# Scores and weighted values made for two steps together, and the depthwise sums moved from PSUM to SBUF, in a two-layer convolution and attention kernel

## The chip, the core and the metric

The kernel runs on one NeuronCore of one Trainium2 chip. The core has five engines that run their own instruction queues in order: TensorE (PE, matmuls[...]), VectorE (DVE), ScalarE (ACT), GpSimd (POOL) and SyncE (SP, which here issues transfers). The metric is device time in microseconds, median of several runs; lower is better. All arithmetic is in float32.

## What is computed

The input is 8 images of 256 channels and 64 x 64 pixels. Two layers follow each other, each with a group norm ahead of it and a residual add behind it:

```python
x = x + _L0_conv_ref(_gn(x), ...)   # three 1x1 convolutions; two more make 9 weights per pixel and group of
                                    # 8 channels; out = sum over the 9 taps of weight * shifted third map
x = x + _L1_conv_ref(_gn(x), ...)
```

The second layer, around which the change lies, is

```python
att = softmax(einsum(q, unfold7x7(k) + position))          # 4 heads of 64 channels, 49 neighbours of each pixel
out_att = einsum(att, unfold7x7(v))
wts = softmax(einsum('oc,bchw->bohw', Wfc, x) as 9 weights per channel and pixel)
hid = relu(dwconv3x3(x, w1)); oc = dwconv3x3(hid, w2)      # depthwise
out_conv = sum over the 9 of oc * wts
return rate1 * out_att + rate2 * out_conv
```

`oc` is the same for all nine weights. The nine weights sum to one up to rounding; the kernel computes them and their quotient as written.

## The kernel before

**Tiling.** An image is cut into 8 bands of 8 rows (512 pixels). Channels are in two tiles of 128 partitions (`ct`). The main loop (L985) runs over all 64 bands, `g`, and in each band over 8 steps, `s` = (`ct`, `m`) with `m` = 0 to 3. Layer 0 runs ahead: beside layer 1 of band g, layer 0 works on bands g + 9 to g + 12, and its first 12 bands are made alone, with g < 0. In the last ten bands or so, layer 0 has nothing left to do.

**Order.** The order of every queue is the order in which the program text calls the operations (`manual_schedule`, L963). `advance()` moves a counter by one, six times a step, and runs what `after(n, f)` has put off by n such moves. `beside(g, s)` says which operations of layer 0, of the queries, keys and values and of the next band go into the middle or the end of a step.

**A step of layer 1** (L991 to L1039):
- Attention is made in tiles of 8 x 8 queries, two tiles and two heads per step, against 14 x 14 keys. `scores` (L694) makes 8 PE matmuls (L703) of 64 rows, 64 columns and 196 keys into `sco`, a PSUM tile of two banks, one per head. DVE adds the mask and takes the row maximum (L712); ACT makes exponentials with row sums (L720); DVE takes the reciprocal (L727); ACT scales (L729). One step later PE transposes these probabilities (`transposed`, L735) and ACT copies them to SBUF (L737). Another step later 16 small PE matmuls (`weighted_values`, L747) multiply them with the values. Their result, 128 columns, lies in the same `sco` tile as the new step's scores, in columns 256 to 383 of the first bank. `add_values` (L757, DVE) adds it to the output rows.
- `branch_weights` (L825) makes two of the eight weight differences of the nine-fold softmax (the ninth is taken off beforehand, L200): four PE matmuls 128 x 128 x 512 and, on ACT, two exponentials (L830). POOL sums them over the steps (L1026). After the fourth step `dynamic_sum` (L832) divides by the sum and multiplies with `oc` (POOL: L838, L855 to L857; DVE: L845, L846, L850).
- The depthwise convolutions are nine taps each. ACT makes the middle tap (L773, L802) and DVE adds the eight others, each an instruction `sum = input * weight + sum` over one band (L782, L808), two in the first half of a step and two in the second. `m` = 0 and 1 do the first convolution, 2 and 3 the second. The sum `acc` is a PSUM tile of one bank. `relu` (L788) and the scaling by rate2 (L818, `depthwise_end`), both on ACT, bring it to SBUF (`hid`, `oc`). In bands with i = 0 the first row is made apart, with taps of its own.

**Layer 0 beside it.** For each of 9 taps, DVE multiplies a PSUM tile of weights with a map (L460), and POOL adds the product (L468). `hidden_maps` (L409) has a convolution of its own on PE (L429), in two parts, put off by 13 and 19 moves.

**PSUM.** [...] `sco` 2, `acc` 1, and 5 for all else (`gen`).

Of the kernel before, what the change touches and what calls it, by code (L numbers as in the profile page):

```python
# [10 lines left out]
F32 = mybir.dt.float32  # L11
# [75 lines left out]
def conv_layers_kernel(ctx: ExitStack, tc: tile.TileContext, ins: dict, out: bass.AP):  # L87
# [77 lines left out]
        nc.vector.tensor_scalar(bq[:, ct : ct + 1], chan[:, ct, CBQ : CBQ + 1], HD**-0.5, None, ALU.mult)  # L165

    rate1, rate2 = rowp[:, RR1 : RR1 + 1], rowp[:, RR2 : RR2 + 1]
    bv = const.tile([P, NCT], F32, name="bv")
    for ct in range(NCT):
        nc.vector.tensor_mul(bv[:, ct : ct + 1], chan[:, ct, CBV : CBV + 1], rate1)  # L170
# [44 lines left out]
    def after(n, f):  # L215
        later.append((place[0] + n, f))
# [103 lines left out]
    def small_maps(b, i):  # L320


        im = images[b]

        p12 = ps.tile([P, R // 2, W], F32, tag="gen", name=f"p12_{b}_{i}", bufs=5)
        for kt in range(NCT):
            for u in range(2):
                nc.tensor.matmul(
                    p12[64 * u : 64 * u + 64], im.w12s[:, kt, :],
                    im.xc[i][:, kt, u * BAND // 2 : (u + 1) * BAND // 2],  # L330
                    start=(kt == 0), stop=(kt == NCT - 1),
                )
        return lambda: write_maps(b, i, p12)
# [360 lines left out]
    def scores(b, i, ct, m, sco):  # L694


        im = images[b]
        qb, kb = im.qb[i, ct], im.kb[i, ct]
        nm = f"{b}_{i}_{ct}_{m}"
        for t in range(2):  # L700
            for h in range(2):
                c0 = (2 * m + t) * TQ
                nc.tensor.matmul(  # L703
                    sco[half[t], h, :NKEY], qb[half[h], 2 * m + t].rearrange("p r c -> p (r c)"),
                    kb[half[h], :, c0 : c0 + KW], start=True, stop=True,
                )

        prob = probs[turn[0] % len(probs)]
        turn[0] += 1
        nmax = w1.tile([P, 2], F32, tag="nmax", name=f"nmax_{nm}", bufs=4)  # L710
        for h in range(2):
            nc.vector.tensor_tensor_reduce(  # L712
                prob[:, h, :NKEY], sco[:, h, :NKEY], mask, -1.0, 3.0e38, ALU.add, ALU.min, nmax[:, h : h + 1]
            )
        return prob, nmax

# [20 lines left out]
        nc.scalar.copy(pt, ptp)  # L737
        return pt

    def weighted_values(b, i, ct, m, pt, sco):  # L740
        im = images[b]
        po = sco[:, 0, 256 : 256 + 2 * NQ].rearrange("p (r c) -> p r c", r=R)
        for t in range(2):
            for ch in range(2):
                n = min(R, WP - (i + ch) * R) * KW
                for h in range(2):
                    nc.tensor.matmul(  # L747
                        po[half[h], :, t * TQ : (t + 1) * TQ],
                        im.vt[i + ch, m][:n, t, (2 * ct + h) * HD : (2 * ct + h + 1) * HD],
                        pt[:n, h, ch, t * NQ : (t + 1) * NQ],  # L750
                        start=(ch == 0), stop=(ch == 1),
                    )
        return po

    def add_values(b, i, ct, m, po):
        x = images[b].xr[i][:, ct].rearrange("p (r c) -> p r c", r=R)[:, :, 2 * m * TQ : 2 * (m + 1) * TQ]
# [3 lines left out]
    def depthwise_begin(b, i, ct):  # L760


        im = images[b]
        r0 = i * R
        nm = f"{b}_{i}_{ct}"
        yp = im.yp[i]
        lo, hi = (r0 + 1 if i else 0), min(r0 + R + 1, H)
        hid = im.hid[i, ct] = w1.tile([P, R + 2, W], F32, tag="hid1", name=f"hid1_{nm}", bufs=3)
        if i:
            nc.scalar.copy(hid[:, 0:2], im.hid[i - 1, ct][:, R : R + 2])  # L770
        for ra0, rb0 in ((lo, lo + 1), (lo + 1, hi)) if i == 0 else ((lo, hi),):
            acc = ps.tile([P, R, W], F32, tag="acc", name=f"acc1_{nm}_{ra0}")
            nc.scalar.activation(  # L773
                acc[:, : rb0 - ra0], yp[:, ct, PAD + ra0 - r0 : PAD + rb0 - r0], AF.Copy,
                scale=chan[:, ct, CW1 + 4 : CW1 + 5],
            )

            def tap(k, acc=acc, ra0=ra0, rb0=rb0):
                ra, rb, ca, cb = taps(ra0, rb0, k // 3, k % 3)
                o = acc[:, ra - ra0 : rb - ra0, ca:cb]  # L780
                dr, dc = k // 3 - 1 + PAD - r0, k % 3 - 1
                nc.vector.scalar_tensor_tensor(  # L782
                    o, yp[:, ct, ra + dr : rb + dr, ca + dc : cb + dc],
                    chan[:, ct, CW1 + k : CW1 + k + 1], o, ALU.mult, ALU.add,
                )

            def relu(acc=acc, ra0=ra0, rb0=rb0):
                nc.scalar.activation(hid[:, ra0 - r0 + 1 : rb0 - r0 + 1, :], acc[:, : rb0 - ra0], AF.Relu)  # L788

            ks = [k for k in range(KK) if k != 4 and taps(ra0, rb0, k // 3, k % 3)[0] < taps(ra0, rb0, k // 3, k % 3)[1]]  # L790
            if rb0 < hi:
                for k in ks:
                    tap(k)
                relu()
        return [lambda k=k: tap(k) for k in ks], relu

    def depthwise_middle(b, i, ct):

        r0 = i * R
        hid = images[b].hid[i, ct]  # L800
        acc = ps.tile([P, R, W], F32, tag="acc", name=f"acc2_{b}_{i}_{ct}")
        nc.scalar.activation(acc, hid[:, 1 : R + 1, :], AF.Copy, scale=chan[:, ct, CW2 + 4 : CW2 + 5])  # L802

        def tap(k):
            ra, rb, ca, cb = taps(r0, r0 + R, k // 3, k % 3)
            o = acc[:, ra - r0 : rb - r0, ca:cb]
            dr, dc = k // 3 - r0, k % 3 - 1
# [5 lines left out]
        return [lambda k=k: tap(k) for k in range(KK) if k != 4], acc  # L813

    def depthwise_end(b, i, ct, acc):

        oc = w1.tile([P, BAND], F32, tag="oc", name=f"oc_{b}_{i}_{ct}")
        nc.scalar.activation(oc, acc.rearrange("p r c -> p (r c)"), AF.Copy, scale=rate2)  # L818
        return oc

    def branch_weights(b, i, ct, m, j, ex):

# [46 lines left out]
    def beside(g, s):  # L869
# [93 lines left out]
    with tc.manual_schedule():  # L963
# [21 lines left out]
        for g in range(-AHEAD, B * NB):  # L985
            b, i = divmod(g, NB)
            for s in range(STEPS):
# [1 line left out]
                mid, end = beside(g, s)  # L989
                steer(g, s)  # L990
                if g >= 0:  # L991
                    if s == 0 and g + AHEAD < B * NB:
                        mid.append(small_maps(*divmod(g + AHEAD, NB)))
# [6 lines left out]
                    pending = [] if before is None else [(before[:-1], transposed(nm, before[-1]))]  # L1000
# [22 lines left out]
                if g >= 0:  # L1023
                    branch_weights(b, i, ct, m, 1, ex)
                    if exb is not None:
                        after(4, lambda ex=ex, exb=exb: nc.gpsimd.tensor_add(ex, ex, exb))  # L1026
                    if m == 1:
                        conv[1]()
                        conv = depthwise_middle(b, i, ct)
                    if m == NT // 2 - 1:  # L1030
                        oc = depthwise_end(b, i, ct, conv[1])
                        after(4, lambda a=(b, i, ct, ex, oc): dynamic_sum(*a))
                if s % 4 == 3 and 0 <= (g * NCT + ct + 1) < B * NB * NCT:
                    gn, cn = divmod(g * NCT + ct + 1, NCT)
                    conv = depthwise_begin(*divmod(gn, NB), cn)
# [2 lines left out]
                    f()  # L1038
                advance()  # L1039
        for last in (before, None):  # L1040
            sco = score_tile(f"end{last is None}")
            weighted = [(a, weighted_values(*a, pt, sco)) for a, pt in pending]
            for a, po in weighted:
# [86 lines left out]
```

## Time and profile before

| what | value |
|---|---|
| time, median of 3 runs | 4152.74 us (4151.52 to 4157.1) |
| span of the profiled run | 4150.9 us, 72735 instructions |
| ACT | 3081.0 us busy (74%) |
| L825, PE, weight differences | x4096, 1930.5 us busy, 595 ns each |
| L747, PE, weighted values | x8160, 347.0 us busy |
| L703, PE, scores | x4096, 295.2 us busy |
| L782, DVE, first depthwise taps | x1104, 766.2 us busy, 694 ns each |
| L808, DVE, second depthwise taps | x1024, 757.8 us busy, 740 ns each |
| L460, DVE, products of layer 0 | x576, 733.9 us busy, 1281 ns each |
| transfers | 367.89 MB, mean 89 GB/s |

A line of the profile's groups names the source line, the engine, the operation, output and inputs by tile names, shapes, how often it ran, then busy time and mean duration of one, and last the time that the engine was idle just before these instructions, with what ended it. The busy time of a matmul overlaps that of the next, since matmuls are pipelined; what PE really spends per matmul is seen in the starts of the timeline. The duration of an instruction runs from its start on the engine to its end, whatever it did in between.

### The profile page before, as it was taken

The page shows a single profiled execution, that of the slowest core. Times are in us where ns is not written, and L with a number is a line of the kernel's source. Part 1 is how long each engine was busy: PE and PEld are TensorE (multiplying, and loading weights), DVE is VectorE, ACT ScalarE, POOL GpSimd, SP SyncE. Part 2 cuts the span into 40 slices and gives each one's busy share as a digit, 9 for nine tenths or more (in the row PEclk, how much of TensorE's full clock was granted, in tenths as well). Part 3 has the DMA queues.
Part 4 walks back from the last instruction along what each step waited for, and adds up shares of the span by engine and source line. Part 5 has one row for each costly group of instructions (what it writes and reads, how often), then busy time and mean ns, then how long its engine had stood idle before and what let it go on. Part 6 is the DMA issues. An engine that isn't in the chain of part 4 may idle for free.

```text
span 4150.9 us, 72735 instructions
## 1 busy us (share of the span) xinstructions
PE 4022.6 (97%) x25292; PEld 2126.8 (51%) x25292; DVE 3591.9 (87%) x7248; ACT 3081.0 (74%) x7726; POOL 2923.0 (70%) x1902
## 2 busy tenths in 40 slices
PE   6789999999999999999999999999999999999998
PEld 3345555555555555555555555555555555455554
DVE  5878998899898898889998898888988889977777
ACT  3467778777787777877778777777778777687776
POOL 4767777677786777777777777777777677744554
PEclk8999999999999999999999999999999999999999
DMA  8854234234244233334234234244233233111100
GB/s 226 194 135 111 73 91 109 72 94 109 62 101 107 76 94 98 81 94 109 72 85 118 72 94 105 66 101 106 71 82 99 65 87 85 33 41 39 39 28 21
DMA packets 381264, 367.89 MB, mean 89 GB/s; under 512 B 55648, under 2 KB 282720, under 8 KB 380640
## 3 DMA queue, kind: packets, MB, share of 16 engines
q1 hardware_dynamic: 377568, 358.68, 34.3%
q8 instruction: 200, 3.28, 0.3%
q10 hardware_dynamic: 3328, 4.55, 0.3%
q14 instruction: 168, 1.38, 0.1%
HBM read 261.42 MB, written 101.71 MB: 87 GB/s over the span
## 4 chain that ended last, share of the span: by engine, by line
PE 71%; DVE 14%; POOL 6%; ACT 5%; DMA 2%; issue 2%; SPq 1%; POOLq 0%; ACTq 0%; DVEq 0%
PE pf L825 33%; PE ptp L735 5%; PE sco L747 5%; PE pk L658 5%; PE sco L703 5%; PE p L369 5%; DVE prod L460 4%; PE pq L637 4%; POOL xg L468 3%; PE pvt L607 2%; PE pv L563 2%; DVE acc L808 2%; PE pw L447 2%; DVE acc L782 2%; POOL ex L1026 2%
## 5 line engine op out<-in xcount | busy, mean ns | idle before, releaser
L825 PE MATMUL pf<-yp,c_wfc 128*128 128x512 f32 x4096 | 1930.5, 595 | 10.6 <-ACT vc L581 5.0
L468 POOL TENSOR_TENSOR xg<-xg,prod 128x1024 f32<-128x1024 f32 x549 | 1203.9, 2193 | 96.6 <-DVE prod L460 64.1
L825 PEld LDWEIGHTS pf<-yp,c_wfc 128*128 128x128 f32 x4096 | 729.9, 190 | 690.5 <-issue 619.4
L1026 POOL TENSOR_TENSOR ex<-ex,ex 128x1024 f32<-128x1024 f32 x384 | 907.7, 2364 | 61.9 <-ACT ex L830 57.2
L830 ACT ACTIVATE ex<-pf 128x512 f32<-128x512 f32 x1024 | 607.3, 593 | 297.9 <-POOL ex L1026 141.3
L782 DVE SCALAR_TENSOR_TENSOR acc<-yp,c_chan,acc 128x504 f32<-128x504 f32 (+3 forms) x1104 | 766.2, 694 | 42.3 <-ACT acc L773 21.7
L460 DVE SCALAR_TENSOR_TENSOR prod<-pw,c_par,x3q 128x1040 f32<-128x1040 f32 x576 | 733.9, 1281 | 66.8 <-PE pw L447 21.6
L808 DVE SCALAR_TENSOR_TENSOR acc<-hid,c_chan,acc 128x504 f32<-128x504 f32 (+3 forms) x1024 | 757.8, 740 | 20.2 <-ACT acc L802 2.1
L855 POOL TENSOR_TENSOR ex<-ex,rec 128x512 f32<-128x512 f32 x127 | 162.3, 1278 | 809.5 <-DVE rec L850 767.1
L729 ACT ACTIVATE prob<-prob,tot 128x196 f32<-128x196 f32 x1024 | 411.6, 450 | 387.2 <-DVE tot L727 386.4
L712 DVE CUSTOM_DVE_ANT_0 prob<-sco,c_mask 128x196 f32<-128x196 f32 x1024 | 325.5, 355 | 272.4 <-PE sco L703 272.0
L720 ACT ACTIVATE prob<-prob,nmax 128x196 f32<-128x196 f32 x1024 | 461.4, 454 | 46.9 <-DVE nmax L712 45.3
L747 PEld LDWEIGHTS sco<-pt,vt 112*64 112x64 f32 x8160 | 283.8, 137 | 182.3 <-issue 51.7
L737 ACT COPY pt<-ptp 112x512 f32<-112x512 f32 x511 | 297.0, 581 | 105.0 <-PE ptp L735 103.0
L735 PE MATMUL ptp<-ident,prob 128*112 128x128 f32 x2044 | 341.7, 287 | 31.2 <-ACT prob L729 30.5
L747 PE MATMUL sco<-pt,vt 112*64 112x64 f32 x8160 | 347.0, 227 | 0.0
L735 PEld LDWEIGHTS ptp<-ident,prob 128*112 128x112 f32 x2044 | 203.9, 133 | 201.4 <-issue 77.7
L703 PE MATMUL sco<-kb,qb 64*64 64x196 f32 x4096 | 295.2, 357 | 0.0
L563 PE MATMUL pv<-yp,c_wv 128*128 128x512 f32 (+2 forms) x576 | 247.3, 554 | 0.6
L369 PE MATMUL p<-xc,w3s 128*128 128x512 f32 x512 | 244.4, 601 | 0.0
L658 PE MATMUL pk<-yp,c_wk 128*128 128x512 f32 (+2 forms) x576 | 240.8, 545 | 0.0
L637 PE MATMUL pq<-yp,c_wq 128*128 128x512 f32 x512 | 240.6, 592 | 0.0
(140 smaller groups left out, 5294.0 us busy)
## 6 DMA issues: line engine op xcount, KB each, us to landing
x<-x3n SPq DMA_DIRECT2D x128, 264.0 KB, 2.1
x3q<-x SPq DMA_DIRECT2D x128, 264.0 KB, 7.2
xc<-in_x SPq DMA_DIRECT2D x64, 512.0 KB, 5.0
xg<-in_x SPq DMA_DIRECT2D x256, 128.0 KB, 4.8
x<-xg SPq DMA_DIRECT2D x256, 128.0 KB, 2.4
yp<-x SPq DMA_DIRECT2D x128, 256.0 KB, 3.3
xr<-x SPq DMA_DIRECT2D x64, 512.0 KB, 5.8
out_x<-xr SPq DMA_DIRECT2D x64, 512.0 KB, 3.1
```

Of the source, the lines that this page charges most:

```text
L369: nc.tensor.matmul(p3, im.w3s[:, kt, mt * P : (mt + 1) * P], im.xc[i][:, kt, :], start=(kt == 0), stop=(kt == NCT - 1),)
L460: nc.vector.scalar_tensor_tensor(prod[:, :, :RUN], pw[:, j, :RUN].unsqueeze(1).to_broadcast([P, SHARE, RUN]), par[:, PCB2 + k : PCB2 + k + 1],
L468: nc.gpsimd.tensor_add(im.xg[i], im.xg[i], rows(prod))
L703: nc.tensor.matmul(sco[half[t], h, :NKEY], qb[half[h], 2 * m + t].rearrange("p r c -> p (r c)"), kb[half[h], :, c0 : c0 + KW], start=True, ...
L720: nc.scalar.activation(prob[:, h, :NKEY], prob[:, h, :NKEY], AF.Exp, bias=nmax[:, h : h + 1], scale=-1.0, accum_out=tot[:, h : h + 1],)
L735: nc.tensor.transpose(ptp[:, h, ch], prob[:, h, ch * CHUNK : (ch + 1) * CHUNK], ident)
L747: nc.tensor.matmul(po[half[h], :, t * TQ : (t + 1) * TQ], im.vt[i + ch, m][:n, t, (2 * ct + h) * HD : (2 * ct + h + 1) * HD], pt[:n, h, ch ...
L782: nc.vector.scalar_tensor_tensor(o, yp[:, ct, ra + dr : rb + dr, ca + dc : cb + dc], chan[:, ct, CW1 + k : CW1 + k + 1], o, ALU.mult, ALU.add,
L808: nc.vector.scalar_tensor_tensor(o, hid[:, ra + dr : rb + dr, ca + dc : cb + dc], chan[:, ct, CW2 + k : CW2 + k + 1], o, ALU.mult, ALU.add,)
L825: nc.tensor.matmul(pf, wfc[:, kt, 2 * m + j, ct * P : (ct + 1) * P], images[b].yp[i][:, kt, PAD : PAD + R], start=(kt == 0), stop=(kt == N ...
L830: nc.scalar.activation(ex[:, j].rearrange("p (r c) -> p r c", r=R), pf, AF.Exp)
L1026: after(4, lambda ex=ex, exb=exb: nc.gpsimd.tensor_add(ex, ex, exb))
```

## The change

Three things are done together. Scores are made for two steps at once, in every second step: `sco` now holds two times 196 columns per head, and the row maximum of the second step is taken one step later from the same tile. Weighted values are also made for two steps at once, right behind the scores, into a tile `po` of their own. The purpose is fewer switches of PE between kinds of small matmuls. The bank for `po` is got by taking the depthwise sums out of PSUM: they are now summed in SBUF, in `hid` and `oc` themselves, with ReLU in place on `hid`; rate2 is multiplied into the second convolution's weights beforehand, so `depthwise_end` goes. The first row of an image is no longer made apart. In `beside`, the second part of layer 0's hidden convolution is put off by 25 in place of 19 moves, so that it comes ahead of a step with scores.

```diff
+    for ct in range(NCT):
+        nc.vector.tensor_scalar(chan[:, ct, CW2 : CW2 + KK], chan[:, ct, CW2 : CW2 + KK], rate2, None, ALU.mult)
...
-                    sco[half[t], h, :NKEY], qb[half[h], 2 * m + t].rearrange("p r c -> p (r c)"),
+                    score_of(sco, h, m)[half[t]], qb[half[h], 2 * m + t].rearrange("p r c -> p (r c)"),
...
+    def score_of(sco, h, m):
+        return sco[:, h, m % 2 * NKEY : (m % 2 + 1) * NKEY]
...
-        po = sco[:, 0, 256 : 256 + 2 * NQ].rearrange("p (r c) -> p r c", r=R)
+        po = po[:, m % 2]
...
+        po = ps.tile([P, 2, R, 2 * TQ], F32, tag="po", name=f"po_{nm}")
+        return [(a, weighted_values(*a, pt, po)) for a, pt in steps]
...
-            acc = ps.tile([P, R, W], F32, tag="acc", name=f"acc1_{nm}_{ra0}")
...
+        new = hid[:, lo - r0 + 1 : hi - r0 + 1]
+        nc.scalar.activation(
+            new, yp[:, ct, PAD + lo - r0 : PAD + hi - r0], AF.Copy, scale=chan[:, ct, CW1 + 4 : CW1 + 5]
+        )
+        def tap(k):
+            ra, rb, ca, cb = taps(lo, hi, k // 3, k % 3)
+            o = hid[:, ra - r0 + 1 : rb - r0 + 1, ca:cb]
...
+        return [lambda k=k: tap(k) for k in range(KK) if k != 4], lambda: nc.scalar.activation(new, new, AF.Relu)
...
-        acc = ps.tile([P, R, W], F32, tag="acc", name=f"acc2_{b}_{i}_{ct}")
+        oc = w1.tile([P, BAND], F32, tag="oc", name=f"oc_{b}_{i}_{ct}")
+        acc = oc.rearrange("p (r c) -> p r c", r=R)
...
-    def depthwise_end(b, i, ct, acc):
...
-            at = (3, 7, 8, 12, 16) if alone else (5, 13, 14, 19, 21)
+            at = (3, 7, 8, 12, 16) if alone else (5, 13, 14, 25, 27)
...
-                    sco = score_tile(nm)
-                    weighted = [(a, weighted_values(*a, pt, sco)) for a, pt in pending]
-                    prob, nmax = scores(b, i, ct, m, sco)
+                    weighted = []
+                    if m % 2 == 0:
+                        sco = score_tile(nm)
+                        for e in range(2):
+                            scores(b, i, ct, m + e, sco)
+                        weighted, pending = weigh_steps(nm, pending), []
+                        if s == 0 and g + AHEAD < B * NB:
+                            mid.append(small_maps(*divmod(g + AHEAD, NB)))
+                        if before is not None:
+                            pending.append((before[:-1], transposed(nm, before[-1])))
+                    prob, nmax = masked(nm, m, sco)
...
+                    if m % 2:
+                        pending.append((before[:-1], transposed(nm, before[-1])))
```

More of the change, by code (lines that the diff above doesn't have):

```diff
@@ L698, in scores @@
         qb, kb = im.qb[i, ct], im.kb[i, ct]
-        nm = f"{b}_{i}_{ct}_{m}"
         for t in range(2):
@@ L703, in scores, with masked @@
                 nc.tensor.matmul(
-                    sco[half[t], h, :NKEY], qb[half[h], 2 * m + t].rearrange("p r c -> p (r c)"),
+                    score_of(sco, h, m)[half[t]], qb[half[h], 2 * m + t].rearrange("p r c -> p (r c)"),
                     kb[half[h], :, c0 : c0 + KW], start=True, stop=True,
                 )
+    def score_of(sco, h, m):
+        return sco[:, h, m % 2 * NKEY : (m % 2 + 1) * NKEY]
+    def masked(nm, m, sco):
         prob = probs[turn[0] % len(probs)]
@@ L712, in scores @@
             nc.vector.tensor_tensor_reduce(
-                prob[:, h, :NKEY], sco[:, h, :NKEY], mask, -1.0, 3.0e38, ALU.add, ALU.min, nmax[:, h : h + 1]
+                prob[:, h, :NKEY], score_of(sco, h, m), mask, -1.0, 3.0e38, ALU.add, ALU.min, nmax[:, h : h + 1]
             )
@@ L738, in transposed, with weighted_values @@
         return pt
-    def weighted_values(b, i, ct, m, pt, sco):
+    def weighted_values(b, i, ct, m, pt, po):
         im = images[b]
-        po = sco[:, 0, 256 : 256 + 2 * NQ].rearrange("p (r c) -> p r c", r=R)
+        po = po[:, m % 2]
         for t in range(2):
@@ L753, in weighted_values, with weigh_steps @@
         return po
+    def weigh_steps(nm, steps):
+        if not steps:
+            return []
+        po = ps.tile([P, 2, R, 2 * TQ], F32, tag="po", name=f"po_{nm}")
+        return [(a, weighted_values(*a, pt, po)) for a, pt in steps]
     def add_values(b, i, ct, m, po):
@@ L770, in depthwise_begin @@
             nc.scalar.copy(hid[:, 0:2], im.hid[i - 1, ct][:, R : R + 2])
-        for ra0, rb0 in ((lo, lo + 1), (lo + 1, hi)) if i == 0 else ((lo, hi),):
-            acc = ps.tile([P, R, W], F32, tag="acc", name=f"acc1_{nm}_{ra0}")
-            nc.scalar.activation(
-                acc[:, : rb0 - ra0], yp[:, ct, PAD + ra0 - r0 : PAD + rb0 - r0], AF.Copy,
-                scale=chan[:, ct, CW1 + 4 : CW1 + 5],
-            )
[L778 to L795, printed above, removed]
+        new = hid[:, lo - r0 + 1 : hi - r0 + 1]
[5 more added lines that the diff above has]
+            o = hid[:, ra - r0 + 1 : rb - r0 + 1, ca:cb]
+            dr, dc = k // 3 - 1 + PAD - r0, k % 3 - 1
+            nc.vector.scalar_tensor_tensor(
+                o, yp[:, ct, ra + dr : rb + dr, ca + dc : cb + dc],
+                chan[:, ct, CW1 + k : CW1 + k + 1], o, ALU.mult, ALU.add,
+            )
+        return [lambda k=k: tap(k) for k in range(KK) if k != 4], lambda: nc.scalar.activation(new, new, AF.Relu)
     def depthwise_middle(b, i, ct):
@@ L811, in tap @@
             )
-        return [lambda k=k: tap(k) for k in range(KK) if k != 4], acc
-    def depthwise_end(b, i, ct, acc):
-        oc = w1.tile([P, BAND], F32, tag="oc", name=f"oc_{b}_{i}_{ct}")
-        nc.scalar.activation(oc, acc.rearrange("p r c -> p (r c)"), AF.Copy, scale=rate2)
-        return oc
+        return [lambda k=k: tap(k) for k in range(KK) if k != 4], oc
     def branch_weights(b, i, ct, m, j, ex):
@@ L991, in conv_layers_kernel @@
                 if g >= 0:
-                    if s == 0 and g + AHEAD < B * NB:
-                        mid.append(small_maps(*divmod(g + AHEAD, NB)))
                     nm = f"{b}_{i}_{ct}_{m}"
-                    sco = score_tile(nm)
-                    weighted = [(a, weighted_values(*a, pt, sco)) for a, pt in pending]
-                    prob, nmax = scores(b, i, ct, m, sco)
+                    weighted = []
[9 more added lines that the diff above has]
+                    prob, nmax = masked(nm, m, sco)
                     for a, po in weighted:
                         add_values(*a, po)
-                    pending = [] if before is None else [(before[:-1], transposed(nm, before[-1]))]
                     tot = exponentials(nm, prob, nmax)
@@ L1030, in conv_layers_kernel @@
                     if m == NT // 2 - 1:
-                        oc = depthwise_end(b, i, ct, conv[1])
-                        after(4, lambda a=(b, i, ct, ex, oc): dynamic_sum(*a))
+                        after(4, lambda a=(b, i, ct, ex, conv[1]): dynamic_sum(*a))
                 if s % 4 == 3 and 0 <= (g * NCT + ct + 1) < B * NB * NCT:
@@ L1040, in conv_layers_kernel @@
         for last in (before, None):
-            sco = score_tile(f"end{last is None}")
-            weighted = [(a, weighted_values(*a, pt, sco)) for a, pt in pending]
-            for a, po in weighted:
+            for a, po in weigh_steps(f"end{last is None}", pending):
                 add_values(*a, po)
```

## The prediction

> **What bounds the kernel now.** I read the page's first part first (engine totals), then its costliest groups, then the waits of TensorE (PE), then windows by stage, then single instructions of VectorE (DVE) and GpSimd (POOL) side by side in the timeline.
>
> ```profile
> PE 4022.6 (97%) x25292; PEld 2126.8 (51%) x25292; DVE 3591.9 (87%) x7248; ACT 3081.0 (74%) x7726; POOL 2923.0 (70%) x1902
> L468 POOL TENSOR_TENSOR xg<-xg,prod 128x1024 f32<-128x1024 f32 x549 | 1203.9, 2193 | 96.6 <-DVE prod L460 64.1
> L1026 POOL TENSOR_TENSOR ex<-ex,ex 128x1024 f32<-128x1024 f32 x384 | 907.7, 2364 | 61.9 <-ACT ex L830 57.2
> ```
>
> PE is the bound: it runs 97% of the span, and its waits add up to about 111 us, the largest 30.5 us (L735 for ScalarE, L729). DVE at 87% and POOL at 70% are both long, and they run side by side. The windows say how long in the steady part (columns: stretch, its length, then busy time of PE, PEld, DVE, ACT, POOL):
>
> ```profile
> 2000.00:3000.00 1000.00, 988.32 (x6318) 527.07 (x6313) 896.85 (x1811) 772.88 (x1940) 748.15 (x482) 1.00 0.36 91
> 3650.00:4100.00 450.00, 449.15 (x2814) 231.69 (x2813) 341.94 (x813) 337.71 (x904) 220.84 (x142) 1.00 0.10 34
> ```
>
> A band (8 steps, one g) begins with its score matmuls, L703: the first ever at 246.3 us, those of band 54 at 3611.8. So 54 heavy bands take 62.3 us each, and the last 10, in which layer 0 has no work left, about 53.4 each. A heavy band holds 0.748 x 62.3 = 46.6 us of POOL and 0.897 x 62.3 = 55.9 us of DVE; a light one 26.2 and 40.6.
>
> The decisive view is DVE against POOL, instruction by instruction. First POOL, then DVE, in one stretch:
>
> ```profile
> 1476.31 1.27 POOL L838 TENSOR_TENSOR ex<-ex 128x512 f32<-128x512 f32 x1
> 1477.54 2.23 POOL L468 TENSOR_TENSOR xg<-xg,prod 128x1024 f32<-128x1024 f32 x1
> ```
>
> ```profile
> 1476.16 0.24 DVE L296 TENSOR_SCALAR w12s<-c_w,sc_a 128x64 f32<-128x64 f32 x1
> 1476.32 1.41 DVE L297 TENSOR_SCALAR w3s<-c_w,sc_a 128x256 f32<-128x256 f32 x1
> 1477.65 2.17 DVE L296 TENSOR_SCALAR w12s<-c_w,sc_a 128x64 f32<-128x64 f32 x1
> ```
>
> The same 64-element instruction takes 0.24 us once and 2.17 us the next time, and the long one ends when the POOL instruction of that moment ends (1477.54 + 2.23 = 1479.77). DVE stood still behind POOL, and the page counts that as busy. Note the order: after L297, POOL's next instruction got in before DVE's next one. The reverse holds too, with a DVE instruction that reads two tensors in SBUF:
>
> ```profile
> 60.30 2.28 DVE L200 TENSOR_TENSOR c_wfc<-c_wfc,last 128x2048 f32<-128x2048 f32 x1
> 60.36 4.25 POOL L468 TENSOR_TENSOR xg<-xg,prod 128x1024 f32<-128x1024 f32 x1
> ```
>
> L468 takes 4.25 us in place of its median of 2.19, and the excess, 2.06, is what was left of L200.
>
> [...] That a two-input DVE instruction is also held up by a running POOL instruction is not in this trace[...]. [...] 692 ns for 512 elements all in SBUF (L856 on DVE, POOL idle), 753 for the depthwise tap with its sum in PSUM.
>
> In the kernel before, every large two-tensor DVE instruction of the steady part has one input in PSUM: taps (acc), products (pw), scores (sco), keys (pk), values (sco). That is why 87% of DVE and 70% of POOL fit together.
>
> **The change, part by part.**
>
> *Scores and weighted values in pairs (PE).* The work is the same: 8 score matmuls and 16 weighted-value matmuls per step. What goes is half the switches between array shapes. In PE's timeline four 128x512 matmuls take 1.72 us to the next group's start (2008.34 to 2010.06), but 1.81 us ahead of L747 (2004.92 to 2006.73): a switch costs about 0.09 us. A step has three (into L747, to L703, to L735); I take 0.09 for each. Removed: 3 x 0.09 in every second step, 256 x 0.27 = 69 us. It is on the path as long as PE is the bound. `po` in a bank of its own costs nothing: add_values reads it two steps ahead of the next pair.
>
> *Second convolution of layer 0 (+19 to +25, +21 to +27).* Its last four matmuls move from ahead of an odd step to ahead of an even one, where the shape changes anyway. No cost; their result is first read in the next band.
>
> *rate2 folded into the second taps.* Two small DVE instructions at the start, hidden behind the constants' loads; 128 ACT instructions of 687 ns (L818), 88 us, go. ACT is at 74% and not the bound: nothing.
>
> *First row no longer apart.* 80 short taps of some 0.29 us (L782, 128x63 and 128x64), 23 us of DVE, go in bands with i = 0. ACT now writes sums into SBUF, some 0.1 us dearer (L788 611 ns, L374 688): nothing.
>
> *Depthwise sums in SBUF.* This sets the time. A tap, of mean 744 ns for 504 elements, loses the PSUM extra, 753 - 692 = 61 ns: 0.684. 32 taps per band: 23.8 us becomes 21.9. But each now reads two SBUF tensors (yp or hid, and the sum), so it excludes any POOL tensor instruction. Per heavy band [...] 46.6 (POOL) + 21.9 (taps) + 0.8 (two L845) = 69.3 us, over the band's 62.3. That alone is +7.0 x 54 = 378 us: 4530 is the floor with perfect interleaving.
>
> How badly do they interleave? DVE's queue has the taps in pairs, 16 per band. The first of a pair comes upon POOL at work with a share u, and waits for half a running instruction, weighted by length: with 9 x 2.19, 6 x 2.36 and 8 x 1.27 us per band, 0.5 x 89.6/44.1 = 1.02 us. The second finds, with a chance q, that POOL's next instruction slipped in between, as at 1477.54, and waits for all of it, 44.1/23 = 1.92 us on average. So DVE waits W = 16 x (1.02 u + 1.92 q) per band. POOL's 46.6 us are done in these waits or beside DVE's other work (55.9 - 23.8 = 32.1 us): u = (46.6 - W)/32.1. Hence W = (23.7 + 30.7 q)/1.51, and the band is T = 32.1 + 21.9 + W. The bounds are q = 0 (W 15.7, T 69.7) and q = 1 (W 36.1, T 90.1). I take q = 0.5, since POOL has its next instruction ready for part of the time only (25% of that stretch it is idle): W 25.9, T 79.9, +17.6 x 54 = 950 us. In the light bands the same sum (6 x 2.36 and 8 x 1.27, other DVE work 16.8) gives W 19.7 and T 58.4: +5 x 10 = 50. Sum: 4153 + 950 + 50 = 5150.
>
> Who waits behind a blocked tap: DVE's queue is in order, so the row maximum of the next step (L712), the reciprocal (L727), the products (L460) and the keys come late; behind L712 wait ACT's exponentials and then PE's transposes, and `sco` is freed late, so PE stands at the next scores with all that follows in its queue. PE's 69 us are then hidden in its new idle time.
>
> **Rivals.**
>
> 1. *Taps blocked, in pairs as worked out* (0.80): 5150, between 4550 and 5770 for q from 0 to 1. For it: the three stretches above. Against it: no tap-against-POOL pair exists yet.
> 2. *Strict alternation* (0.07): all of POOL's work passes while taps wait, T = 32.1 + 21.9 + 46.6 = 100.6; 4153 + 38.3 x 54 + 115 = 6340. For it: POOL took its turn between two DVE instructions at 1477.54. Against it: POOL also runs beside the other 32 us.
> 3. *No blocking by this kind of instruction* (0.10): PE stays the bound, 4153 - 69 = 4084, and the cheaper taps (123 + 23 us of DVE) do not show. For it: the trace shows only POOL held by a two-input instruction, and only once. Against it: that once is a clean 2.06 us.
> 4. *Interleaving so good that it costs a little more than PE saves, or PE's gain and the waits cancel* (0.03, most of it within 0.2%): 4150 to 4530. Against it: 69.3 us do not fit into 62.3.
>
> **How the numbers follow.** The likeliest is 1, and its centre, 5150, is the prediction. The range takes q from 0 to 1, 4550 to 5770; outside are rivals 2, 3 and 4, two in ten. Faster 0.10 (rival 3), same 0.02, slower 0.88.
>
> **What would show it.** Right: mean of the tap groups (now on hid and oc) not 0.7 but 1.2 to 1.8 us, with a minimum near 0.68; POOL's L468 mean over 2.19; DVE's share up to some 95%, PE's down to about 80%, with PE idle ahead of the scores for DVE; bands of some 80 us up to band 54 and under 60 after it. Wrong: taps of 0.68 us throughout and bands of 61 us, which is rival 3; or bands near 100 us. The switch price is seen in the starts of PE's groups: one run of three switches per two steps.

## The result, and the profile after

The changed kernel takes 5319.51 us (median of 4 runs, 5316.46 to 5323.5), the kernel before 4152.47 us: a ratio of 1.281, 95% interval 1.279 to 1.283. It is 1167 us slower, at 5320 where 5150 was forecast, within the range. Line numbers below are those of the kernel named; most have moved by 2 to 20 lines. In the changed kernel the first convolution's taps are L793, the second's L812, layer 0's adds on POOL L470, the row add L770, and POOL's last multiply and add of `dynamic_sum` L854 and L855.

The engine totals and the costliest groups of the changed kernel:

```profile
PE 4322.9 (81%) x25292; PEld 2314.2 (44%) x25292; DVE 4785.9 (90%) x7170; ACT 2980.5 (56%) x7566; POOL 3216.9 (61%) x1902
L812 DVE SCALAR_TENSOR_TENSOR oc<-hid,c_chan,oc 128x504 f32<-128x504 f32 (+3 forms) x1024 | 1728.7, 1688 | 18.1
L470 POOL TENSOR_TENSOR xg<-xg,prod 128x1024 f32<-128x1024 f32 x549 | 1251.1, 2279 | 627.8 <-DVE prod L462 581.5
L1031 POOL TENSOR_TENSOR ex<-ex,ex 128x1024 f32<-128x1024 f32 x384 | 1035.8, 2697 | 225.1 <-ACT ex L828 225.1
L793 DVE SCALAR_TENSOR_TENSOR hid<-yp,c_chan,hid 128x504 f32<-128x504 f32 (+6 forms) x1024 | 1027.9, 1004 | 18.1
```

DVE has fewer instructions than before, 7170 against 7248, and 1194 us more busy time. The taps alone rose from 766.2 + 757.8 = 1524 us to 1027.9 + 1728.7 = 2757 us, +1233, with nearly no idle time before them: the time is inside the instructions. POOL's two adds became longer too (2193 to 2279 ns, 2364 to 2697 ns), with the same number of instructions. The chain of work that ended last was mostly PE's in the kernel before and is DVE's now (shares of the span by engine, first before, then after):

```profile
PE 71%; DVE 14%; POOL 6%; ACT 5%; DMA 2%; issue 2%; SPq 1%; POOLq 0%; ACTq 0%; DVEq 0%
```

```profile
DVE 69%; PE 10%; POOL 9%; issue 4%; ACT 4%; DMA 2%; SPq 1%; POOLq 0%; DVEq 0%; ACTq 0%
```

The windows of a stretch with layer 0 beside it and of one without (columns as before: stretch, its length, then busy time of PE, PEld, DVE, ACT and POOL; the first number after these is PE's granted clock, as a share of full speed):

```profile
2000.00:3000.00 1000.00, 811.96 (x4810) 437.86 (x4809) 917.17 (x1351) 570.48 (x1458) 624.41 (x364) 0.92 0.28 70
4800.00:5250.00 450.00, 410.34 (x2521) 215.81 (x2518) 390.91 (x722) 290.85 (x788) 221.33 (x128) 0.98 0.09 29
```

The first scores start at 244.4 us, those of band 54 at 4709.6: heavy bands take 82.7 us (62.3 before), the last ten 59.3 (53.4 before). 54 x 20.4 + 10 x 5.9 = 1161 us, which is the loss but for a few us. So nearly all of it arises while layer 0 runs beside layer 1.

Now DVE's timeline in one stretch, then POOL's:

```profile
2332.78 0.61 DVE L770 SCALAR_TENSOR_TENSOR xr<-po,bv,xr 128x128 f32<-128x128 f32 x2 [2.42 <-POOL xr L855]
2333.31 1.29 DVE L462 SCALAR_TENSOR_TENSOR prod<-pw,c_par,x3q 128x1040 f32<-128x1040 f32 x1
2334.52 3.49 DVE L812 SCALAR_TENSOR_TENSOR oc<-hid,c_chan,oc 128x504 f32<-128x504 f32 x2
2337.93 0.15 DVE L733 RECIPROCAL tot<-tot 128x2 f32<-128x2 f32 x1
2338.04 3.66 DVE L812 SCALAR_TENSOR_TENSOR oc<-hid,c_chan,oc 128x504 f32<-128x504 f32 x2
```

```profile
2331.48 1.27 POOL L855 TENSOR_TENSOR xr<-xr,oc 128x512 f32<-128x512 f32 x1
2332.70 4.75 POOL L470 TENSOR_TENSOR xg<-xg,prod 128x1024 f32<-128x1024 f32 x2
2337.42 2.80 POOL L1031 TENSOR_TENSOR ex<-ex,ex 128x1024 f32<-128x1024 f32 x1
```

Read the last pair of taps first. It starts at 2338.04, while L1031 runs. L1031 ends at 2340.22; two bare taps of 0.74 from there on would end at 2341.70, and the pair does end at 2338.04 + 3.66 = 2341.70. That fits a first tap that stood still until POOL was done. The pair at 2334.52 has the same pattern in its second tap: the second L470 ends at 2332.70 + 4.75 = 2337.45, and the pair ends 0.56 us later, at 2338.01. Ahead of both stands something the prediction did not have: L770 waits 2.42 us for POOL's L855.

The waits, largest of those that matter (engine and line waiting, releaser, then total us, times, longest):

```profile
POOL ex L853 <- DVE rec L848: 733.1, 120, 11.5
POOL xg L470 <- DVE prod L462: 581.5, 242, 8.8
PE sco L704 <- DVE kb L675: 303.7, 96, 5.6
DVE xr L770 <- POOL xr L855: 300.9, 127, 3.6
PE ptp L741 <- ACT qb L643: 152.9, 54, 4.2
PE ptp L741 <- ACT prob L735: 125.4, 69, 4.9
```

DVE is late, so PE waits for DVE's keys and, through ACT, for the probabilities (ACT itself waits 1363.3 us in all for DVE's reciprocal L733); POOL waits for DVE's products, of which before it missed 64 us and now misses 582.

### The profile page after: what moved, and what is told of

The parts are those of the page before. It is cut to its first block, busy times and chain, and to the rows that moved or that the text cites. A ratio compares the mean times of both kernels' runs of the same rounds, so it can differ in the third digit from the quotient of the medians.

```text
span 5314.5 us, 72361 instructions
## 1 busy us (share of the span) xinstructions
PE 4322.9 (81%) x25292; PEld 2314.2 (44%) x25292; DVE 4785.9 (90%) x7170; ACT 2980.5 (56%) x7566; POOL 3216.9 (61%) x1902
## 4 chain that ended last, share of the span: by engine, by line
DVE 69%; PE 10%; POOL 9%; issue 4%; ACT 4%; DMA 2%; SPq 1%; POOLq 0%; DVEq 0%; ACTq 0%
DVE oc L812 28%; DVE hid L793 14%; DVE prod L462 8%; DVE rec L848 4%; POOL ex L853 3%; POOL xr L855 3%; POOL oc L854 3%; DVE prob L718 3%; PE pf L823 3%; DVE rec L844 3%; PE po L753 2%; DVE ex L843 2%; DVE xr L770 2%; PE sco L704 2%; DVE kb L668 2%
## 5 line engine op out<-in xcount | busy, mean ns | idle before, releaser
L823 PE MATMUL pf<-yp,c_wfc 128*128 128x512 f32 x4096 | 2001.9, 618 | 63.1 <-DVE prod L462 41.4
L812 DVE SCALAR_TENSOR_TENSOR oc<-hid,c_chan,oc 128x504 f32<-128x504 f32 (+3 forms) x1024 | 1728.7, 1688 | 18.1
L470 POOL TENSOR_TENSOR xg<-xg,prod 128x1024 f32<-128x1024 f32 x549 | 1251.1, 2279 | 627.8 <-DVE prod L462 581.5
L735 ACT ACTIVATE prob<-prob,tot 128x196 f32<-128x196 f32 x1024 | 413.4, 451 | 1363.3 <-DVE tot L733 1363.3
L1031 POOL TENSOR_TENSOR ex<-ex,ex 128x1024 f32<-128x1024 f32 x384 | 1035.8, 2697 | 225.1 <-ACT ex L828 225.1
L823 PEld LDWEIGHTS pf<-yp,c_wfc 128*128 128x128 f32 x4096 | 781.6, 201 | 894.6 <-issue 710.9
L793 DVE SCALAR_TENSOR_TENSOR hid<-yp,c_chan,hid 128x504 f32<-128x504 f32 (+6 forms) x1024 | 1027.9, 1004 | 18.1
L853 POOL TENSOR_TENSOR ex<-ex,rec 128x512 f32<-128x512 f32 x127 | 162.6, 1280 | 779.3 <-DVE rec L848 733.1
L770 DVE SCALAR_TENSOR_TENSOR xr<-po,bv,xr 128x128 f32<-128x128 f32 x509 | 154.3, 344 | 314.5 <-POOL xr L855 300.9
L753 PE MATMUL po<-pt,vt 112*64 112x64 f32 x8144 | 344.5, 246 | 1.0
L753 PEld LDWEIGHTS po<-pt,vt 112*64 112x64 f32 x8144 | 304.7, 158 | 92.6 <-issue 89.7
L660 PE MATMUL pk<-yp,c_wk 128*128 128x512 f32 (+2 forms) x576 | 317.9, 688 | 28.2 <-DVE d_a L251 13.0
L704 PEld LDWEIGHTS sco<-kb,qb 64*64 64x64 f32 x4096 | 155.0, 148 | 396.7 <-issue 362.8
```

Of the source, the lines that this page charges most:

```text
L470: nc.gpsimd.tensor_add(im.xg[i], im.xg[i], rows(prod))
L704: nc.tensor.matmul(score_of(sco, h, m)[half[t]], qb[half[h], 2 * m + t].rearrange("p r c -> p (r c)"), kb[half[h], :, c0 : c0 + KW], start ...
L753: nc.tensor.matmul(po[half[h], :, t * TQ : (t + 1) * TQ], im.vt[i + ch, m][:n, t, (2 * ct + h) * HD : (2 * ct + h + 1) * HD], pt[:n, h, ch ...
L793: nc.vector.scalar_tensor_tensor(o, yp[:, ct, ra + dr : rb + dr, ca + dc : cb + dc], chan[:, ct, CW1 + k : CW1 + k + 1], o, ALU.mult, ALU.add,
L812: nc.vector.scalar_tensor_tensor(o, hid[:, ra + dr : rb + dr, ca + dc : cb + dc], chan[:, ct, CW2 + k : CW2 + k + 1], o, ALU.mult, ALU.add,)
L823: nc.tensor.matmul(pf, wfc[:, kt, 2 * m + j, ct * P : (ct + 1) * P], images[b].yp[i][:, kt, PAD : PAD + R], start=(kt == 0), stop=(kt == N ...
```

## Experiments

Each ratio is against the kernel before, run on the same chip. **The theory:** the loss comes from taps with two SBUF inputs and POOL's tensor instructions shutting each other out. **The rival:** it comes from the new order, scores and weighted values in pairs, which delays the softmax.

**e1, the pairs alone; e2, the SBUF sums alone; e3, the SBUF sums with one SBUF input.** e1 keeps the sum in PSUM and takes `po` from the five `gen` banks; e2 is the kernel before with the new depthwise code only; e3 is e2 with one operand changed: each tap adds a row of zeros in PSUM in place of the running sum, so the summing over the taps is left out.

```diff
e1:
-            acc = oc.rearrange("p (r c) -> p r c", r=R)
+            acc = ps.tile([P, R, W], F32, tag="acc", ...)
-        po = ps.tile([P, 2, R, 2 * TQ], F32, tag="po", name=f"po_{nm}")
+        po = ps.tile([P, 2, R, 2 * TQ], F32, tag="gen", name=f"po_{nm}", bufs=5)
e3, against e2, in both convolutions:
-                chan[:, ct, CW1 + k : CW1 + k + 1], o, ALU.mult, ALU.add,
+                chan[:, ct, CW1 + k : CW1 + k + 1], zero_like(rb - ra, ca, cb), ALU.mult, ALU.add,
```

> Scores and weighted values in pairs as in the changed kernel, but the depthwise sums in PSUM (acc) as before; the pair's weighted values take one of the five rotating gen banks. Theory (taps with two SBUF inputs and POOL shut each other out): no such tap is left, so taps last 0.74 us and never 2.5, TensorE is the bound again and saves its switches, 4153 - 69 = 4084; up to 4130 if the row adds, which now come behind POOL's last step in program order, wait for it. Rival (the pairing itself, with its late row adds and later frees, makes the changed kernel slow): above 4500.

> Before with the depthwise sums in SBUF and nothing else (rate2 folded into the weights, first row not apart, no pairing). Theory: nearly all of the 1167 us, less the row adds' wait for POOL (301 us in the changed kernel), which comes with the pairing: 5000 to 5300, taps bimodal at 0.74 and about 2.5 us. Rival (pairing is the cause): about 4150.

> As the run with the sums alone in SBUF, same outputs, same order, but each tap's second input is a row of zeros in PSUM in place of the running sum, so that it reads one SBUF tensor; it still writes SBUF. The summing over the taps is left out. Theory[...]: taps 0.74 us and unimodal, time 4100 to 4170. Rival (writing the sums into SBUF, or waiting for them there, is what collides): 5000 or more, taps still at 2.5 us.

| kernel | us | ratio (95%) |
|---|---|---|
| e1, pairs only | 4233.27 | 1.019 (1.0175 to 1.0206) |
| e2, SBUF sums only | 5254.14 | 1.264 (1.2622 to 1.2664) |
| e3, SBUF sums, one SBUF input | 4126.88 | 0.993 (0.9915 to 0.9944) |

The second taps' group in e2, then in e3 (busy time, mean ns of one):

```profile
L801 DVE SCALAR_TENSOR_TENSOR oc<-hid,c_chan,oc 128x504 f32<-128x504 f32 (+3 forms) x1024 | 1962.8, 1917 | 21.9 <-ACT oc L795 3.7
```

```profile
L807 DVE SCALAR_TENSOR_TENSOR oc<-hid,c_chan,zero 128x504 f32<-128x504 f32 (+3 forms) x1024 | 749.8, 732 | 20.5 <-ACT oc L801 2.2
```

The SBUF sums by themselves cost 1098 us. With the same count of taps, all writing SBUF, and only the second input read from PSUM, all of it is gone. So it is neither the place of the output nor the order. e3 changes one thing more: its taps no longer depend on one another through the sum. That waiting for the sum in SBUF is not the cause is shown by m1, below.

The pairs alone were expected to gain. They cost 77 us, a miss. e1's waits offer a reason, which e5 takes away:

```profile
DVE xr L768 <- POOL xr L868: 289.4, 127, 3.6
PE ptp L739 <- ACT vc L581: 76.2, 42, 3.0
PE pf L836 <- DVE xr L768: 29.5, 24, 1.5
```

The row add again waits for POOL, here holding one of the five `gen` banks, and PE waits behind it (third line).

**e4 and e5, the row add ahead of POOL.** Before, the add of step (ct 0, m 3) stood one step earlier in DVE's queue than POOL's last add into the same rows. In pairs it comes behind it. Both runs call `weigh`, which holds POOL's last three instructions, one move later, so that the pair's adds stand ahead of them again; e4 in the changed kernel, e5 in e1.

```diff
-            after(2, weigh)
+            after(3, weigh)
```

> The changed kernel with the last three POOL instructions of the dynamic sum put off by one more move, so that the row adds of the pair stand ahead of them in program order and need not wait for POOL. Theory (that wait is part of the cost of its own): the 301 us of VectorE's idle time vanish and some of it comes back as longer blocking of taps, 5030 to 5200. Rival (VectorE's wait only lets POOL do work that would otherwise block taps): within 60 us of 5319.

> Pairs of steps with the depthwise sums in PSUM, as in the run with the pairs only, and the last three POOL instructions of the dynamic sum put off by one move, so that the row adds stand ahead of them. Theory (the 80 us that pairs alone lost are VectorE's 289 us of waiting for POOL at the row adds, which reach TensorE): the wait is gone, and the switches saved show: 4084, between 4070 and 4110, and faster than before. Rival (pairs lose for another reason, such as gen banks short of one or scores that come late): 4150 or more.

e4 takes 5104.46 us (1.228, 1.2265 to 1.2301), 215 us less than the changed kernel. Idle time of DVE ahead of the row add, first in the changed kernel, then in e4:

```profile
  POOL xr L855: 300.9, 127
```

```profile
  PE po L753: 6.6, 19
```

So this order is worth 215 us of the 1167. DVE's 300.9 us of idle time for POOL are gone, but part of them came back inside the taps, whose means rose to 1714 (L812) and 1032 ns (L793). The edit moves more than the row add, though: POOL's own wait for the reciprocal (L853) fell from 733.1 to 178.0 us, and its wait for the products (L470) rose from 581.5 to 1063.3. What the row add's wait alone costs was not measured.

e5 takes 4238.12 us (1.020, 1.0183 to 1.0211), no better than e1. The row add's wait for POOL is gone. PE's wait in the first line was there in e1 too (76.2); the one in the second line came up (13.8 in e1):

```profile
PE ptp L739 <- ACT vc L581: 92.8, 42, 3.3
ACT ex L841 <- POOL oc L867: 286.4, 114, 3.6
```

In e1, then, taking the row add's wait for POOL away brought nothing: it is not what the pairs lose there, or another wait took its place.

**m1, the tap by itself.** A kernel of its own, run once, with groups of eight instructions on 128 x 512 elements, alone and beside eight POOL adds of 128 x 1024. Its form, for the blocked case and the four that vary it:

```python
pool_adds(); scalar_tensor_tensor(o, a, w, o)        # two SBUF inputs, SBUF out
pool_adds(); scalar_tensor_tensor(acc, a, w, o)      # two SBUF inputs, PSUM out
pool_adds(); scalar_tensor_tensor(o, a, w, acc)      # one SBUF input, SBUF out
pool_sets(); scalar_tensor_tensor(o, a, w, o)        # POOL writes only
tensor_add(o, a, o)                                  # no scalar operand, POOL idle
```

> Not the layers at all: only loops of eight depthwise-like instructions of VectorE on 128 x 512, each group alone or beside a queue of POOL instructions, and copies of x to the output; everything else is left out. With POOL idle: sum in SBUF, sum in PSUM, plain two-input add in SBUF. Theory after the result: 0.75, 0.75, 0.69 us (the scalar operand costs, not PSUM); the prediction's step said 0.69 for the first. With POOL adding 128 x 1024: two SBUF inputs alternate one for one with POOL, mean near 0.75 + 2.2, with the output in SBUF or PSUM alike; one SBUF input and one in PSUM stays at 0.75, with the output in SBUF or PSUM alike; beside POOL instructions that only write (memset), two SBUF inputs stay at 0.75. Rival[...]: the group with one SBUF input that writes SBUF is blocked too, and the memsets block.

Groups, in the order: these five, then the tap alone with SBUF sum and with PSUM sum (after the bar: busy us, mean ns):

```profile
L68 DVE SCALAR_TENSOR_TENSOR o<-a,w,o 128x512 f32<-128x512 f32 x8 | 19.9, 2491 | 0.2
L80 DVE SCALAR_TENSOR_TENSOR acc<-a,w,o 128x512 f32<-128x512 f32 x8 | 19.9, 2482 | 0.2
L76 DVE SCALAR_TENSOR_TENSOR o<-a,w,acc 128x512 f32<-128x512 f32 x8 | 6.0, 747 | 0.2
L84 DVE SCALAR_TENSOR_TENSOR o<-a,w,o 128x512 f32<-128x512 f32 x8 | 6.0, 751 | 0.2
L64 DVE TENSOR_TENSOR o<-a,o 128x512 f32<-128x512 f32 x8 | 5.5, 691 | 0.2
L58 DVE SCALAR_TENSOR_TENSOR o<-a,w,o 128x512 f32<-128x512 f32 x8 | 6.0, 752 | 2.5 <-DMA a<-in_x 2.3
L61 DVE SCALAR_TENSOR_TENSOR acc<-a,w,acc 128x512 f32<-128x512 f32 x8 | 6.0, 755 | 0.2
```

And the blocked group beside POOL's in the timeline:

```profile
24.72 20.18 DVE L68 SCALAR_TENSOR_TENSOR o<-a,w,o 128x512 f32<-128x512 f32 x8
25.54 21.56 POOL L49 TENSOR_TENSOR ga<-ga,gb 128x1024 f32<-128x1024 f32 x8
```

Eight taps that need 6.0 us alone take 19.9 us here, with both queues always ready. The first starts ahead of the adds; if it took its bare 0.75 us, the other seven took 2.74 each, and an add of this group takes 21.56/8 = 2.70. By this estimate about one add passes per tap, and in the terms of the prediction q is near 1. It makes no difference whether the output lies in PSUM or SBUF (2482 and 2491 ns), a tap with one SBUF input stays at 747, and a POOL that only writes does not block the tap (751). The plain add with two SBUF inputs is blocked beside POOL's adds as well (2475 ns). m1 also settles what e3 left open: the second group is blocked though its taps do not read what they write, and the fourth is not blocked though each of its taps adds to the sum of the one before. The bare tap costs the same with its sum in SBUF (752) and in PSUM (755); only the plain add is cheaper (691).

**e6, e7, e8: what pairs and banks are worth.** e6 and e7 are the changed kernel and the kernel before with no DVE taps, e8 is the kernel before with four `gen` banks.

```diff
e6, e7, in both convolutions:
         def tap(k):
+            return
e8:
-        ..., tag="gen", ..., bufs=5)
+        ..., tag="gen", ..., bufs=4)
```

> The changed kernel with all depthwise taps on VectorE left out (the middle taps on ScalarE stay). Theory: no tap is left to collide, TensorE is the bound, and what the pairing with a bank of its own saves is seen against the next run: it is faster by 50 to 75 us (256 x 0.27 = 69). Rival (pairing costs by its order even where VectorE has room): as slow as the next run, or slower.

> Before with all depthwise taps on VectorE left out. TensorE was the bound, so little should go: 4110 to 4150 (it waits some 111 us in all, most of it early). This is what the changed kernel without taps is compared with.

> Before with four rotating gen banks in place of five, one bank unused. Theory for the pairs with sums in PSUM (they lost 80 us because po takes one of the five gen banks for part of the time): 4190 to 4260. Rival (the lost time comes from the order of the row adds and the exponentials, not from the bank): under 4170.

e6 takes 3983.97 us (0.959, 0.9572 to 0.96), e7 4072.68 (0.980, 0.9782 to 0.9815): with DVE's taps out of the way, pairs with a bank of their own are worth 88.7 us, 0.35 us per pair of steps. That is more than the 50 to 75 expected. The two kernels also differ in ACT's part of the depthwise sums, which e7 still makes in PSUM; ACT is busy 75 and 76% in them, and what this difference is worth was not tried. e7 was expected at 4110 or more; the PSUM taps cost the kernel before 83 us although PE was busy 97% of it. e8 takes 4242.78 us (1.021, 1.0193 to 1.0224), as expected: taking one of the five rotating banks away costs 87 us.

**e9, e10, e11: the pairs without SBUF sums, again.** e9 gives e1's `po` a bank of its own and leaves `gen` four; e10 adds e4's edit; e11 is e1 with no DVE taps.

```diff
e9, e10:
-        po = ps.tile([P, 2, R, 2 * TQ], F32, tag="gen", name=f"po_{nm}", bufs=5)
+        po = ps.tile([P, 2, R, 2 * TQ], F32, tag="po", name=f"po_{nm}")
-        ..., tag="gen", ..., bufs=5)
+        ..., tag="gen", ..., bufs=4)
e10:
-            after(2, weigh)
+            after(3, weigh)
e11, in both convolutions:
         def tap(k):
+            return
```

> Pairs of steps, depthwise sums in PSUM as before, po in a bank of its own and four rotating gen banks in place of five. If the two prices measured apart simply add (one bank less +87, pairing with a bank of its own -89): 4140 to 4170, a tie with before; with the row adds' wait for POOL on top up to 4230. Theory for the pairs-only run (po held a bank out of the ring's turn): below its 4233. Rival (pairs lose because everything behind them comes late once VectorE is loaded): 4230 or more.

> The same with the dynamic sum's last three POOL instructions put off by one move. Theory: no wait of VectorE for POOL at the row adds, nothing else touched, 4120 to 4160. Rival: as with the run of pairs in gen banks, the wait only moves elsewhere and the time stays within 15 us of the run without it.

> Pairs with po among the five rotating gen banks, as in the pairs-only run, and all depthwise taps on VectorE left out. The two runs without taps gave 4073 (no pairs) and 3984 (pairs, po in a bank of its own beside five). If po's place among the five banks is what cost the pairs-only run its gain, it costs it here too: 4060 or more. If VectorE's load is (its late row adds, maxima and products), it does not show here: under 4010.

| kernel | us | ratio (95%) |
|---|---|---|
| e9, own bank, four `gen` | 4399.91 | 1.058 (1.0567 to 1.0599) |
| e10, as e9, row add first | 4425.99 | 1.064 (1.0626 to 1.0662) |
| e11, e1 without taps | 4078.09 | 0.982 (0.9798 to 0.9833) |

e9 and e10 are misses: the price of a bank (87) and the gain of the pairs (89) do not add. e9 is 242 us above the kernel before and some 155 above e8, which has four banks and no pairs. In e10 the row add in front made it 26 us slower still. PE's largest wait in e9:

```profile
PE pf L836 <- ACT qb L641: 115.3, 54, 3.1
```

PE waits for a `gen` bank that ACT has not yet emptied. Why e9 loses so much more than e8 was not settled.

e11 settles a part of e1. Without taps DVE is busy 54%, and still e11 is 94 us above e6; against e7 the pairs gain nothing (+5). So with `po` among the five rotating banks the gain of the pairs is gone even where DVE has room. PE's wait in e11 that e6 does not have:

```profile
PE pq L637 <- DVE xr L768: 62.8, 35, 1.8
```

With DVE's taps, e1 is 77 us above the kernel before in place of 5: the rest of its loss comes only with these taps; by what route, e5 did not show.

No kernel tried that computes everything beats the kernel before. e6's 3984 us is about what the pairs could reach if the taps cost neither a bank nor DVE's time.

## Why the prediction was right, and where it was off

**The mechanism: right.** The taps now read two SBUF tensors each, and such a tap "excludes any POOL tensor instruction". The trace before showed one side of this, POOL held up by L200 (L468 4.25 us in place of 2.19); that a tap is held up by POOL was the author's assumption. e2, e3 and m1 show it: the second taps average 1917 ns in e2 and 732 in e3, and the tap of m1 takes 2491 ns beside POOL's adds and 752 alone. "Any" was too wide, since beside POOL's memsets it takes 751. The sums alone cost 1098 us, and the pairs on top of them another 65. One reading on the way was a little off: L468's excess of 2.06 us was said to be what was left of L200, which is 60.30 + 2.28 - 60.36 = 2.22.

**The heavy band: 79.9 forecast, 82.7 measured.** By term, in the stretch 2000 to 3000 us, where taps take 200.75 + 332.73 us of DVE in 388 instructions, and the rest of DVE 917.17 - 533.48 = 383.7, each times 0.0827 (a band is 82.7 us of the stretch's 1000). W is what the taps took beyond 0.744 us each:

| term, us per heavy band | forecast | measured |
|---|---|---|
| other DVE work | 32.1 | 31.7 |
| 32 bare taps | 21.9 | 23.8 (0.744 each) |
| waiting behind POOL, W | 25.9 | 20.3 |
| DVE idle | 0 | 6.9 |
| sum | 79.9 | 82.7 |

Three terms were mis-sized, and partly cancel. That the sum came within 3 us is thus in part luck.

- *Bare taps.* The step "loses the PSUM extra, 753 - 692 = 61 ns" compared a tap with a plain add. In m1 what differs is the form, a multiplication by a scalar operand and an add in one: 752 ns with the sum in SBUF, 755 in PSUM, 691 for the plain add. So the tap had no PSUM extra to lose. An unblocked tap stayed at 744 ns, the median of L793.
- *W.* The shares u (a pair's first tap comes upon POOL at work) and q (POOL slips in ahead of the second) were guessed as one for all taps: u = (46.6 - 25.9)/32.1 = 0.64 and q = 0.5, which makes a mean wait of 0.65 us for a first tap and 0.96 for a second. The two convolutions differ. Between 1000 and 4500 us, POOL was at work at the start of 28% of L793's firsts and 75% of L812's. Of L793, 14% of the firsts and 28% of the seconds lasted over 1 us, of L812 47% and 60%. Beyond 0.744 us, L793's firsts and seconds took 0.22 and 0.36 us on average, L812's 0.86 and 1.15. So the second convolution waits a little longer than forecast and the first much less: while its taps run, POOL often stands still, waiting for DVE's reciprocal (L853, 733.1 us in all).
- *Idle.* The step "`po` in a bank of its own costs nothing: add_values reads it two steps ahead of the next pair" looked at the bank and at PE, not at the queue of DVE in which the add stands, and not at what else writes the rows that it adds to. L770 waits 300.9 us for POOL in all, and in the stretch 2000 to 3000 us 52.2, which is 4.3 us per band of the 6.9 idle; the order without this wait is worth 215 us (e4). This is the prediction's real miss: a dependence between two additions to one tile, turned over by the pairing.

**Light bands:** 58.4 forecast, 59.3 measured.

**ACT's sums in SBUF.** They were to be "some 0.1 us dearer", an estimate from two instructions (L788, L374) that both write SBUF, which did not show it. For 128x512, ACT's middle taps went from 696 and 692 ns (L773, L802) to 723 each (L785, L806), and ReLU, which now reads SBUF as well, from 611 to 646 (L798): about 0.03 us.

**POOL is held up as well.** The model counted POOL's work at its old 46.6 us; in the same stretch it is 0.624 x 82.7 = 51.6.

**PE.** Three switches at 0.09 gave 0.27 us per pair; e7 less e6 gives 0.35. In the timeline a pair's scores take 0.85 and its weighted values 1.09 us; before, from 2006.73 to 2007.85, one step took 0.51 and 0.61, two steps thus 1.02 and 1.22. After the change:

```profile
2328.16 0.92 PE L704 MATMUL sco<-kb,qb 64*64 64x196 f32 x16
2329.01 1.15 PE L753 MATMUL po<-pt,vt 112*64 112x64 f32 x32
2330.10 0.65 PE L741 MATMUL ptp<-ident,prob 128*112 128x128 f32 x4
```

The step "PE's 69 us are then hidden in its new idle time" is not contradicted. The changed kernel is 65 us above e2, which has no pairs, but e4, which has the row add in front, is 150 us below it. That looks like a gain of the pairs larger than the 89 of e7 less e6. DVE's account says otherwise: it is busy 95% of the span in both, 5012.3 us in e2 and 4835.3 in e4, and idle for 246 and 270, while PE is busy 84 and 83%. The taps alone fell from 3003.7 to 2811.5 us. So e4's lead over e2 lies in shorter waits of the taps behind POOL, not in PE's switches. Why they are shorter was not tried: no run has e4's edit without the pairs.

**The signs named beforehand.** PE at 81% (about 80% was named), DVE at 90% (up to 95%), L470 at 2279 ns (over 2.19), bands as above, one run of switches per two steps: all there. Two others came out differently. The tap means were to be 1.2 to 1.8 us; L812 has 1.69, L793 only 1.00, for the reason under W. And the unblocked tap was to take 0.68 us, and takes 0.74.

**The rivals.** Strict alternation (6340) is what m1 comes near, with both queues always ready; in the kernel POOL is not always ready: it waits 733.1 us for the reciprocal and 581.5 for the products. No blocking (4084) fell with m1 (2491 ns for a tap of 752). Its number would have held for e3 only roughly: 4127, and e3 has no pairs. Near-perfect interleaving (4150 to 4530) fell with the result itself, since the taps of L812 wait about a microsecond each.

## What to carry to other kernels

Before moving an accumulator from PSUM to SBUF, count how many SBUF inputs each VectorE instruction then has, and what GpSimd runs beside it: in this kernel a second one took the taps from 1524 to 2757 us beside GpSimd's work, and in m1 one tap from 0.75 to 2.49 us beside adds that read SBUF. The profile showed the loss as busy time (+1233 us), not as a wait (18.1 us ahead of each of the two groups). When work is batched over two steps, look at each consumer of the batch in its own queue, and ask what else writes the tile that it updates, since its place relative to that writer may turn over. A rotating PSUM bank has a price (87 us in the kernel before), and prices measured apart need not add (e9), so measure in the schedule that will use it.

## What was not expected of the hardware

- The form of the instruction, not the memory of the sum, set the tap's duration in m1: 752 ns in SBUF and 755 ns in PSUM for 512 elements, against 691 ns for an add without the scalar multiplication.
- With both queues full in m1, a tap of 0.75 us took 2.49 us on average beside adds of 128 x 1024, about one add per tap by the estimate above. POOL pays too: eight of these adds took 21.56 us, and 19.26 beside taps with one SBUF input.
- PE's granted clock was lower in two kernels in which PE stood idle more: 0.919 on average after (PE busy 81%) and in e2 (84%), against 0.993 before (97%) and 0.992 in e6 (995 of the 1000 us from 2000 us on). The starts fit this: two `branch_weights` matmuls in a row start 429 ns apart in the median before and after, but 845 to 865 ns apart in 3 of 3107 cases before and 137 of 3214 after. So the changed kernel had stretches in which PE started such matmuls at half the pace. What set the clock was not tried.
